# A graph layer's edge loop: windows of 16 to 80 nodes, sums zeroed by DMA, and three more copied columns on VectorE and ScalarE

## The chip, the core and the metric

The kernel runs on one core of one Trainium2 chip. The time is device microseconds of one launch. The core's engines work in parallel, each through its own list of instructions in order: PE (TensorE, matmul), DVE (VectorE), ACT (ScalarE), POOL (GpSimd) and SP (SyncE, which here only issues DMA). They wait for each other through semaphores. A "q" behind an engine's name, as in DVEq or SPq, means its queue: what is handled before the engine's arithmetic, such as register loads, waits and DMA issues.

## What is computed

The reference is one pre-normed layer of a graph network, with 12500 nodes of 48 values and 400000 edges of 32 values that are sorted by their target node `dst`:

```
h = jnp.maximum(_layernorm(x, axis=-1), 0.0)
x_i = h[dst]
x_j = h[src]
tmp = jnp.concatenate([x_i, x_j, edge_attr], axis=1)
h2 = jax.nn.relu(tmp @ W1 + b1)
msg = h2 @ W2 + b2
x = x + jax.ops.segment_sum(msg, dst, num_segments=12500)
```

The targets are drawn as 12500 u^2 with u uniform, so low nodes have many edges and high nodes few. The sources `src` are uniform.

## The kernel before

First `node_tables` (L102) normalizes the nodes and multiplies them by the two node parts of W1. That makes two tables in DRAM, `tab_a` for targets and `tab_b` for sources, 128 values a row. The table for sources is made a second time, turned, in the core's own memory: `bt`, 128 partitions with one column per node, written by `turn` (L296) in the loop's first iterations, three blocks of 1024 nodes an iteration.

The edges are then taken in 391 chunks of 1024, which are 8 tiles of 128 edges (`windows`, L230). A chunk's targets lie within 80 nodes (`W`). For each chunk:

- SP loads the edge values and, spread over 80 partitions, the target numbers (`lhs`, `row`, L354 and L356), and 80 rows of `tab_a` (`rhs`, L364).
- DVE compares the targets with the 80 node numbers (L379), which makes `lhs` a matrix with a one where an edge meets its target, and counts them in `deg`. It makes the same matrix with edges on partitions, `hot` (L389).
- PE multiplies `lhs` by `rhs` into `pre` (L400): target part and edge part of all 1024 edges. It adds the rows of the sources (L421), which come in one of three ways, below. ACT takes relu of it (`hid`, L437). PE folds the edges onto the chunk's 80 nodes (`p_g`, L445 and L448), and DVE adds that to a piece of the running sums `seg` (L460).

The rows of the sources come in three ways. POOL gathers most tiles from `tab_b` with one indirect DMA per tile of 128 (`gb`, L371; seven buffers of a chunk each). SP fetches the rows of some tiles one by one (`gs`, L289, 15 rows per iteration). And DVE and ACT copy single columns out of `bt` into a turned tile (`gt`, L348): 71 on DVE and 72 on ACT per iteration from iteration 5 on, so that 128 copies make a tile and 430 of the 3125 tiles come that way. A column's address is known only at run time; it is loaded from the table `cols` into the engine's registers by TENSOR_LOAD (L272), a few numbers at a time, ahead of the copies that use them. `PARTS` (L60) lists these parts: five on DVE with 8, 15, 16, 20 and 12 copies and six on ACT with 12, 8, 8, 20, 12 and 12, and `columns` (L325) rounds the number of loaded registers up to a multiple of four; the second part on DVE loads one more, the place of the seg add.

The sums: `seg` has two buffers of 1024 nodes. Twelve chunks make a group (`GQ`, L29; 33 groups and a bit), which uses one buffer. At a change of group DVE zeroes the other buffer with two memsets (L476), loads a number and copies 80 columns of sums over (L478). In the next group's first two iterations PE multiplies the old group's sums by W2 (`p_f`, L488 and L489), DVE adds them to the nodes' values `xseg` (L495), and SP stores those at the group's third (L499).

All runs in a hand-written order: the loop at L502 calls the steps of up to three chunks per iteration, and each engine takes its instructions in just that order. Iteration c prepares chunk c, multiplies chunk c-1 and folds chunk c-2.

Of the kernel before, what the change touches and what calls it, by code (L numbers as in the profile page):

```python
# [28 lines left out]
GQ = 12  # L29
OFF = -(NCH - 3) % GQ  # L30
L = 1024
FAR = L - W
END_L = 4 * W
MID = FAR / 2
BLK = 512
STORE = 2
# [7 lines left out]
HALF = (W - 1) / 2  # L44
# [7 lines left out]
TURNS = 3  # L52
BLOCKS = (NPAD + CE - 1) // CE
BUILD = (BLOCKS + TURNS - 1) // TURNS
COLS = BUILD
# [10 lines left out]
STRIP = 144  # L66
# [4 lines left out]
BASE = 0  # L71

BT0 = 16512
SEG0 = 161696
# [3 lines left out]
AT_PLACE, AT_SEG, SEG, NEXT = 16, 17, 18, 19  # L78
WIDTH = 20
# [13 lines left out]
EPS = 1e-5  # L93

# [135 lines left out]
def windows(nc, tc, gp, bt, ident, idx, raw, rhss, x_t, tab_a, tab_b, dst, edge_t, w2s, b2s,  # L230
            sources, out_t):
# [4 lines left out]
    with ExitStack() as es:  # L236
# [7 lines left out]
        wp = es.enter_context(tc.tile_pool(name="wp", bufs=3))  # L244
        ps_p = es.enter_context(tc.tile_pool(name="ps_p", bufs=2, space=PSUM))
        ps_g = es.enter_context(tc.tile_pool(name="ps_g", bufs=2, space=PSUM))
        ps_f = es.enter_context(tc.tile_pool(name="ps_f", bufs=1, space=PSUM))
        xp = es.enter_context(tc.tile_pool(name="xp", bufs=2))
# [4 lines left out]
        nc.vector.tensor_scalar_add(wnum, wrow, -HALF)  # L253
# [7 lines left out]
        gss = {}  # L261

        def group(c):

            return divmod(c + OFF, GQ)

        def begin(g):
            return max(0, g * GQ - OFF)

# [24 lines left out]
        bt_v = bt.rearrange("h (p r) -> h r p", r=NR)  # L294

        def turn(i):  # L296

            n = min(T, NR - i * T)
            p_t = ps_p.tile([P, T, HID], F32, name="pre")
            parts = p_t.rearrange("h (k q) p -> h k q p", k=2)  # L300
            for k in range(2):
                nc.tensor.matmul(
                    parts[:, k, : n // 2, :].rearrange("h q p -> h (q p)"), wb[:, k, :],
                    ht[: 2 * D, i * T // 2 : (i * T + n) // 2, :].rearrange("k g p -> k (g p)"),
                    start=True, stop=True,
                )
            nc.scalar.copy(
                bt_v[:, i * T : i * T + n, :].rearrange("h (q k) p -> h q k p", k=2),
                parts[:, :, : n // 2, :].rearrange("h k q p -> h q k p"),
            )  # L310
# [14 lines left out]
        def columns(c, part):  # L325
# [15 lines left out]
            for k, of in enumerate(got[:n]):  # L341
                j, e = divmod(first + k, P)
                if j not in gts:
                    gts[j] = gtc.tile([HID, P], F32, name="gt")
                of = of.with_bounds(
                    min_val=BT0, max_val=BT0 + 4 * (N - 1), guaranteed_mod_val=0, out_of_modulus=4
                ) - BT0
                copy(gts[j][:, e : e + 1], bt8[:, bass.ds(of, 4)].bitcast(F32))  # L348

        def prepare(c):  # L350
            n = min(T, NT - c * T)
            at = c * CE
            lhs = ld.tile([P, CE], F32, name="lhs")
# [3 lines left out]
                row[:, : n * P],  # L357
                dst[at : at + n * P].rearrange("(o e) -> o e", o=1).to_broadcast([W, n * P]),
            )
            m = max(0, min(RPART, len(BYROWS) * P - (c - ROWS0) * RPART)) if c >= ROWS0 else 0  # L360
            base, *nodes = numbers(c, BASE, 1 + m, mybir.EngineType.SP)
# [3 lines left out]
                rhs.bitcast(U8)[:W, :],  # L365
                taba8[bass.ds(base, 4 * HID * W)].rearrange("(w h) -> w h", w=W),
# [3 lines left out]
            for t in range(n - len(COLS_OF.get(c, ())) - (c in BYROWS) if c >= RAW else 0):  # L370
# [9 lines left out]
                lhs[:W, : n * P], row[:, : n * P], bw[:, c : c + 1], None,  # L380
                op0=ALU.is_equal, op1=ALU.add, accum_out=deg[:, :1],
# [3 lines left out]
        def compare(c):  # L385

            n = st[c]["n"]
            hot = wp.tile([P, T, W], F32, name="hot")
            nc.vector.tensor_tensor(  # L389
                hot[:, :n, :], wnum.unsqueeze(1).to_broadcast([P, n, W]),  # L390
                rel[:, c * T : c * T + n].unsqueeze(2).to_broadcast([P, n, W]), op=ALU.is_equal,
            )
            st[c]["hot"] = hot
# [46 lines left out]
        def fold(c):  # L440
            s = st[c]
            n = s["n"]
            p_g = ps_g.tile([HID, 2, W], F32, name="p_g")
# [4 lines left out]
            nc.tensor.matmul(p_g[:, 1, :], s["deg"], ident[:W, :W], start=True, stop=True)  # L448
            s["p_g"] = p_g

        def add(c):

            s = st.pop(c)
# [5 lines left out]
            to = segs[k].bitcast(U8)[:, :, bass.ds(at, 4 * W)].bitcast(F32)  # L459
# [4 lines left out]
        def segment_load(g):  # L464

            first, = numbers(begin(g), SEG, 1, mybir.EngineType.SP)
            xs[g] = xp.tile([D, L], F32, name="xseg")
            n = L if begin(g + 1) < NCH else END_L
            nc.sync.dma_start(xs[g][:, :n], x_t[:, bass.ds(node(first), n)])

        def segment_next(g):

            old, new = segs[g % 2], segs[(g + 1) % 2]
            if g > 0:
                for k in range(2):
                    nc.vector.memset(new[:, k, W:], 0.0)  # L476
            of, = numbers(begin(g), NEXT, 1, mybir.EngineType.DVE)
            nc.vector.tensor_copy(  # L478
                new[:, :, :W], old[:, :, bass.ds(of.with_bounds(min_val=0, max_val=FAR), W)]
            )  # L480
# [16 lines left out]
        def segment_store(g, n):  # L497
            first, = numbers(begin(g), SEG, 1, mybir.EngineType.SP)
            nc.sync.dma_start(out_t[:, bass.ds(node(first), n)], xs.pop(g)[:, :n])  # L499

        with tc.manual_schedule():
            for c in range(NCH + 2):  # L502
# [11 lines left out]
                if 0 <= c - 2 < NCH:  # L514
                    add(c - 2)
                    if k == GQ - 1:
# [17 lines left out]
                if k == GQ - 3 or c == NCH - 1:  # L534
# [13 lines left out]
                for i in range(c * TURNS, min((c + 1) * TURNS, BLOCKS)):  # L548
                    turn(i)
# [6 lines left out]
def general(nc, tc, bt, ident, x_t, tab_a, tab_b, src_it, dst_it, dst, edge_t, w1, w2s, b2s,  # L556
            accs, out_t):

    with ExitStack() as es:
# [97 lines left out]
        with tc.tile_pool(name="gfin", bufs=1) as fin, tc.tile_pool(  # L657
            name="g_f", bufs=1, space=PSUM
        ) as ps_f:
            for r0 in range(0, NR, 14):  # L660
                s = slice(r0, r0 + 14)
                got = []
                for k in range(GNACC):
                    a = fin.tile([P, 14, D], F32, name=f"a{k}")
# [7 lines left out]
                for r in range(14):  # L672
# [7 lines left out]
def tile_gnn_preln(  # L680
# [15 lines left out]
    ones: bass.AP,  # L696
    w1: bass.AP,
# [40 lines left out]
    rhss = [const.tile([P, HID], F32, name=f"rhs{k}") for k in range(3)]  # L738
    flag = const.tile([1, 1], I32, name="flag")
# [8 lines left out]
    gp = ctx.enter_context(tc.tile_pool(name="gp", bufs=7))  # L748

    with tc.tile_pool(name="keep", bufs=1) as keep, tc.tile_pool(  # L750
# [14 lines left out]
        def loads():  # L765
# [13 lines left out]
            nc.gpsimd.tensor_scalar_add(b0f, b0f, HALF)  # L779
# [19 lines left out]
        def squares():  # L799
            nc.scalar.activation(bt[:, :NT], rel, AF.Square)  # L800
# [4 lines left out]

        furthest = keep.tile([P, 1], F32, name="furthest")
# [4 lines left out]
        def most():  # L811
# [4 lines left out]
            nc.vector.tensor_scalar(furthest, furthest, HALF * HALF, None, op0=ALU.is_gt)  # L816
# [3 lines left out]
        def check():  # L820
# [7 lines left out]
            nc.vector.tensor_scalar_add(wcol, wcol, -HALF)  # L828
            nc.vector.tensor_scalar(bw, b0f[:W, :], wcol[:W, :], None, op0=ALU.add)

            nc.vector.tensor_scalar(cols, cols, 4, BT0, op0=ALU.mult, op1=ALU.add)
            rows_at = slice(BASE, BASE + 1 + RPART)
# [7 lines left out]
            at = last[:, :, AT_PLACE : AT_PLACE + 1]  # L840
            nc.vector.scalar_tensor_tensor(
                at, last[:, :, AT_SEG : AT_SEG + 1], -4.0, at, op0=ALU.mult, op1=ALU.add
            )
            at_place = slice(PLACE, PLACE + 1)
            nc.vector.scalar_tensor_tensor(
                cols[:, :, at_place], cols[:, :, at_place], 1.0, at, op0=ALU.mult, op1=ALU.add
            )

# [5 lines left out]
    with tc.If(outside == 0) as cmp:  # L854
        windows(nc, tc, gp, bt, ident, (srci, rel, bw, wrow, last, cols, degs), (xg, wb, ht), rhss,
                x_t, tab_a, tab_b, dst16, edge_t, w2s, b2s, sources, out_t)
# [78 lines left out]
```

## Time and profile before

| what | us |
|---|---|
| median of three runs | 3366.36 (3366.21 to 3367.52) |
| the profiled execution | 3372.65 |
| its span in the trace | 3370.8 |
| DVE busy, share of the span | 2800.1, 83% |
| ACT busy | 3035.6, 90% |
| PE busy | 2775.6, 82% |
| POOL busy | 2530.0, 75% |

In a row of groups stand the line, the engine, the instruction, what it writes and reads with partitions and elements, and how often; then busy time, the mean of one in ns, and the idle time of the engine just before, with what ended it. "Issue" there means that the engine waited for nothing that the profile shows. Register loads and waits are not counted as busy. Copies of one column overlap, so their mean duration is longer than the time from one to the next. In a timeline row stand start, length, engine, instruction, count, and in brackets the idle time before it. A row of windows has the stretch, its length, the busy time with the number of instructions in brackets, PE's granted clock, the DMA engines' busy share and GB/s.

### The profile page before, as it was taken

What the parts mean: (1) busy time and instruction counts of PE and PEld (TensorE: products, weight loads), DVE (VectorE), ACT (ScalarE), POOL (GpSimd) and SP (SyncE); (2) the same over time, 40 slices, a digit from 0 to 9 for tenths busy, and PEclk for the clock granted to TensorE, in tenths of its full rate; (3) what the DMA queues carried; (4) which work ended last, traced back from release to release, by engine and by line L of the source; (5) the groups of instructions that cost most, each with busy time, mean ns of one, the idle gap of its engine ahead of it and who ended that gap; (6) DMA issues with size and microseconds to landing.
All of it is one profiled execution on the core that took longest, in us unless ns stands there. A gap on an engine that the chain in (4) does not pass through costs nothing.

```text
span 3370.8 us, 115212 instructions
## 1 busy us (share of the span) xinstructions
PE 2775.6 (82%) x16394; PEld 2158.3 (64%) x16394; DVE 2800.1 (83%) x29140; ACT 3035.6 (90%) x28179; POOL 2530.0 (75%) x2670
## 2 busy tenths in 40 slices
PE   7987778888888888888887788888788788788777
PEld 6666666666666666666666666676666666666565
DVE  6588888888888888888888888888888888888876
ACT  5799998999998999998899999889998999999987
POOL 7677777777777777777777777777777777777776
PEclk9999998998898998988889999888998999899989
DMA  7433333333333333333333333333333333333333
GB/s 262 122 97 104 100 97 100 99 101 100 100 99 100 95 100 102 100 101 97 100 98 101 100 100 102 95 101 97 102 99 98 97 100 98 104 100 97 99 96 83
DMA packets 200234, 349.24 MB, mean 104 GB/s; under 512 B 69219, under 2 KB 107749, under 8 KB 198181
## 3 DMA queue, kind: packets, MB, share of 16 engines
q0 software_dynamic: 84800, 172.53, 18.9%
q1 hardware_dynamic: 114258, 169.09, 16.7%
q14 instruction: 634, 5.19, 0.5%
q8 instruction: 138, 2.26, 0.3%
q10 hardware_dynamic: 404, 0.17, 0.0%
HBM read 322.05 MB, written 22.07 MB: 102 GB/s over the span
## 4 chain that ended last, share of the span: by engine, by line
DVE 71%; issue 14%; PE 5%; DVEq 4%; POOL 2%; DMA 2%; ACT 0%; SPq 0%; POOLq 0%; ACTq 0%
DVE gt L348 47%; DVE lhs L379 12%; DVE hot L389 8%; DVEq L272 4%; DVE seg L460 2%; POOL gb L371 2%; PE pre L400 1%; PE p_g L445 1%; DVE xseg L495 1%; DVE seg L476 1%; DMA row<-in_dst 1%; PE p_f L488 1%; PE p_f L489 1%; DMA gb<-tab_b,srci 1%; PE p_n L195 1%
## 5 line engine op out<-in xcount | busy, mean ns | idle before, releaser
L371 POOL DMA_INDIRECT gb<-tab_b,srci x2618 | 2489.4, 951 | 812.7 <-issue 724.4
L348 ACT COPY gt<-bt 128x1 f32 x27705 | 2618.0, 188 | 63.9 <-issue 54.6
L348 DVE COPY gt<-bt 128x1 f32 x27335 | 1842.1, 144 | 463.3 <-issue 435.1
L400 PEld LDWEIGHTS pre<-rhs,lhs 112*128 112x128 f32 x6250 | 823.5, 208 | 277.1 <-issue 193.4
L400 PE MATMUL pre<-rhs,lhs 112*128 112x128 f32 x6250 | 841.5, 292 | 98.3 <-issue 56.7
L445 PE MATMUL p_g<-hot,hid 128*128 128x80 f32 x6250 | 794.0, 282 | 131.2 <-ACT hid L437 129.1
L445 PEld LDWEIGHTS p_g<-hot,hid 128*128 128x128 f32 x6250 | 758.4, 198 | 164.4 <-ACT hid L437 161.6
L421 PE MATMUL pre<-gb,ident 128*128 128x512 f32 (+2 forms) x1548 | 771.2, 627 | 34.3 <-DMA gb<-tab_b,srci 26.5
L437 ACT ACTIVATE hid<-pre 128x1024 f32<-128x1024 f32 x391 | 397.5, 1017 | 220.2 <-PE pre L421 205.8
L379 DVE TENSOR_SCALAR_CACHE_REDUCE lhs<-row,bw 80x1024 f32<-80x1024 int16 x391 | 494.6, 1265 | 14.8 <-DMA row<-in_dst 14.5
L421 PEld LDWEIGHTS pre<-gb,ident 128*128 128x128 f32 x1548 | 311.8, 225 | 281.0 <-issue 261.7
L421 PE MATMUL pre<-ident,gt 128*128 128x128 f32 x860 | 214.9, 336 | 261.7 <-DVE gt L348 234.7
L421 PEld LDWEIGHTS pre<-ident,gt 128*128 128x128 f32 x860 | 143.8, 210 | 291.5 <-issue 136.4
L389 DVE TENSOR_TENSOR hot<-wnum,rel 128x640 f32<-128x640 f32 x391 | 318.2, 814 | 0.0
L460 DVE TENSOR_TENSOR seg<-seg,p_g 128x160 f32 x391 | 121.5, 311 | 47.8 <-PE p_g L448 47.8
L448 PE MATMUL p_g<-ident,deg 80*128 80x80 f32 x782 | 156.4, 283 | 0.0
L448 PEld LDWEIGHTS p_g<-ident,deg 80*128 80x128 f32 x782 | 123.6, 198 | 0.0
L488 PE MATMUL p_f<-seg,w2s 128*48 128x512 f32 (+1 forms) x134 | 82.2, 700 | 44.3 <-DVE xseg L495 43.9
L489 PE MATMUL p_f<-seg,b2s 1*48 1x512 f32 (+1 forms) x134 | 76.2, 650 | 0.0
L488 PEld LDWEIGHTS p_f<-seg,w2s 128*48 128x48 f32 x134 | 12.3, 135 | 85.9 <-DVE xseg L495 60.0
L476 DVE MEMSET seg<- 128x944 f32 x64 | 54.1, 845 | 9.3
L489 PEld LDWEIGHTS p_f<-seg,b2s 1*48 1x48 f32 x134 | 11.3, 122 | 65.2 <-issue 65.2
(76 smaller groups left out, 429.0 us busy)
## 6 DMA issues: line engine op xcount, KB each, us to landing
gs<-tab_b SPq DMA_DIRECT2D x5760, 0.5 KB
row<-in_dst SPq DMA_DIRECT2D x390, 160.0 KB
lhs<-in_edge_t SPq DMA_DIRECT2D x390, 128.0 KB
gb<-tab_b,srci POOLq DMA_INDIRECT x2618
rhs<-tab_a SPq DMA_DIRECT2D x391, 40.0 KB
xseg<-in_x_t SPq DMA_DIRECT2D x33, 192.0 KB
out_x<-xseg SPq DMA_DIRECT2D x33, 192.0 KB
tab_b<-tab SPq DMA_DIRECT2D x3, 1280.0 KB
```

The costliest lines, as they stand in the source:

```text
L272: return nc.values_load_multi_w_load_instructions(table[c % P : c % P + 1, c // P, at : at + n], engines=[engine], min_val=0, max_val=1 << 23,
L348: copy(gts[j][:, e : e + 1], bt8[:, bass.ds(of, 4)].bitcast(F32))
L371: nc.gpsimd.indirect_dma_start(out=gb[:, t, :], out_offset=None, in_=tab_b[:, :], in_offset=bass.IndirectOffsetOnAxis(ap=srci[:, c * T + t ...
L379: nc.vector.tensor_scalar(lhs[:W, : n * P], row[:, : n * P], bw[:, c : c + 1], None, op0=ALU.is_equal, op1=ALU.add, accum_out=deg[:, :1],)
L389: nc.vector.tensor_tensor(hot[:, :n, :], wnum.unsqueeze(1).to_broadcast([P, n, W]), rel[:, c * T : c * T + n].unsqueeze(2).to_broadcast([P ...
L400: nc.tensor.matmul(pre[:, t, :], s["lhs"][:K, t * P : (t + 1) * P], s["rhs"][:K, :], start=t % BANK == 0, stop=False, skip_group_check=True,)
L421: nc.tensor.matmul(pre[:, t:e, :], lhsT, rhs, start=False, stop=True, skip_group_check=True)
L437: nc.scalar.activation(h[:, :n, :], s["pre"][:, :n, :], AF.Relu)
L445: nc.tensor.matmul(p_g[:, 0, :], s["h"][:, t, :], s["hot"][:, t, :], start=t == 0, stop=t == n - 1)
L448: nc.tensor.matmul(p_g[:, 1, :], s["deg"], ident[:W, :W], start=True, stop=True)
L460: nc.vector.tensor_add(to, to, s["p_g"])
L488: nc.tensor.matmul(p_f[:, :n], w2s, seg[:, 0, s], start=True, stop=False)
```

## The change

- *Spans.* The window of a chunk is 16, 32, 48, 64 or 80 nodes by its place in the edge list (`SPANS`). `hot`, the fold, the seg add, the row transfer, the `rhs` transfer and the partitions of the compare follow that width; the numbers are taken from the window's start, not its middle. `lhs` becomes three fixed buffers, zeroed once at the loop's start, and `rhs` too is zeroed at first. `hot` has two buffers for three. The test that all targets lie in their windows is made per span, by five ACT instructions for one.
- *Groups* have 12 to 103 chunks (`BEGINS`): 15 for 33. The old sums are zeroed by two DMAs on ACT's queue in the group's fifth and seventh iteration (`segment_clear`), not by DVE's memsets; the store comes at the fifth in place of the third.
- *Columns.* DVE's last part has 15 copies for 12, ACT's last too: 74 and 75 per iteration, from iteration 6 on. 447 tiles come that way.
- *Lane order.* `bt` has its columns in the order in which `turn` makes them, so that its copies write contiguous columns, and DVE turns node numbers into columns once, with five more instructions. The turns are spread 2, 2, 2, 2, 3, 2 over six iterations.
- *SP* loads 32 numbers in every second iteration in place of 16 in each.
- *Buffers.* `gb` has eight in place of seven.

```diff
-GQ = 12
+BEGINS = (0, 103, 147, 180, 208, 233, 255, 275, 294, 312, 329, 345, 360, 374, NCH - 5)
-END_L = 4 * W
+END_L = 5 * W
-STORE = 2
+STORE, CLEAR = 4, (4, 6)
+SPANS = ((16, 78), (32, 165), (48, 250), (64, 340), (W, NCH))
-TURNS = 3
+TURNS = (2, 2, 2, 2, 3, 2)
 PARTS = (
-    (True, 0, 8), (True, 8, 15), (True, 24, 16), (True, 40, 20), (True, 60, 12),
-    (False, 72, 12), (False, 84, 8), (False, 92, 8), (False, 100, 20), (False, 120, 12),
-    (False, 132, 12),
+    (True, 0, 8), (True, 8, 15), (True, 24, 16), (True, 40, 20), (True, 60, 15),
+    (False, 76, 12), (False, 88, 8), (False, 96, 8), (False, 104, 20), (False, 124, 12),
+    (False, 136, 15),
 )
...
+        lhss = [one.tile([P, CE], F32, name=f"lhs{k}") for k in range(3)]
+        for lhs in lhss:
+            nc.vector.memset(lhs[:W, :], 0.0)
...
             nc.scalar.copy(
-                bt_v[:, i * T : i * T + n, :].rearrange("h (q k) p -> h q k p", k=2),
+                bt[:, i * CE : i * CE + n * P].rearrange("h (q k p) -> h q k p", k=2, p=P),
...
-            base, *nodes = numbers(c, BASE, 1 + m, mybir.EngineType.SP)
+            if c % 2 == 0:
+                ahead[:] = numbers(c, 0, 2 * RPART + 2, mybir.EngineType.SP)
+            base, nodes = ahead[BASE + c % 2], ahead[c % 2 * RPART :][:m]
...
-                lhs[:W, : n * P], row[:, : n * P], bw[:, c : c + 1], None,
+                lhs[:w, : n * P], row[:w, : n * P], bw[:w, c : c + 1], None,
...
-                hot[:, :n, :], wnum.unsqueeze(1).to_broadcast([P, n, W]),
+                hot[:, :n, :], wnum[:, :w].unsqueeze(1).to_broadcast([P, n, w]),
...
-            to = segs[k].bitcast(U8)[:, :, bass.ds(at, 4 * W)].bitcast(F32)
+            to = segs[k].bitcast(U8)[:, :, bass.ds(at, 4 * w)].bitcast(F32)
...
-            if g > 0:
-                for k in range(2):
-                    nc.vector.memset(new[:, k, W:], 0.0)
...
+        def segment_clear(g, k):
+            nc.scalar.dma_start(
+                segs[g % 2][:, k, W:], zeros.unsqueeze(0).to_broadcast([P, L - W])
+            )
...
-                if g > 0 and k == STORE:
+                if g > 0 and k == (STORE if begin(g + 1) < NCH else 2):
                     segment_store(g - 1, L)
+                if g > 0 and begin(g + 1) < NCH and k in CLEAR:
+                    segment_clear(g - 1, CLEAR.index(k))
...
-    gp = ctx.enter_context(tc.tile_pool(name="gp", bufs=7))
+    gp = ctx.enter_context(tc.tile_pool(name="gp", bufs=8))
```

DVE's instructions of one iteration in the middle of a group, before, from the compare to the next one. `lhs`, `row` and `bw` belong to the compare, `cols` to the register loads, `gt` and `bt` to the column copies.

```order
L379 TENSOR_SCALAR lhs,deg_97<-row,bw 80x1024
L272 TENSOR_LOAD cols
L348 COPY gt<-bt 128x1 x8
L272 TENSOR_LOAD cols
L348 COPY gt<-bt 128x1 x15
L460 TENSOR_TENSOR seg_634<-seg_634,p_g 128x2x80
L272 TENSOR_LOAD cols
L348 COPY gt<-bt 128x1 x16
L389 TENSOR_TENSOR hot<-wnum,rel 128x640
L272 TENSOR_LOAD cols
L348 COPY gt<-bt 128x1 x20
L272 TENSOR_LOAD cols
```

The part that follows this last load has 12 copies before. The same place of the changed kernel, in a stretch with 32 nodes per window, from the last two loads of one iteration on:

```order
L276 TENSOR_LOAD cols
L350 COPY gt<-bt 128x1 x20
L276 TENSOR_LOAD cols
L350 COPY gt<-bt 128x1 x15
L387 TENSOR_SCALAR lhs_661,deg_100<-row,bw 32x1024
L276 TENSOR_LOAD cols
L350 COPY gt<-bt 128x1 x8
L276 TENSOR_LOAD cols
L350 COPY gt<-bt 128x1 x15
L471 TENSOR_TENSOR seg_652<-seg_652,p_g 128x2x32
L276 TENSOR_LOAD cols
```

The order and the five loads are the same; the last part has three copies more, and the compare, hot and the seg add are narrower.

DVE at a change of group, before, from the seg add on:

```order
L460 TENSOR_TENSOR seg_634<-seg_634,p_g 128x2x80
L476 MEMSET seg_635 128x944 x2
L272 TENSOR_LOAD last
L478 ISA
L478 COPY seg_635<-seg_634 128x2x80
L272 TENSOR_LOAD cols
L348 COPY gt<-bt 128x1 x16
```

And in the changed kernel:

```order
L471 TENSOR_TENSOR seg_653<-seg_653,p_g 128x2x32
L276 TENSOR_LOAD last
L486 ISA
L486 COPY seg_652<-seg_653 128x2x80
L276 TENSOR_LOAD cols
L350 COPY gt<-bt 128x1 x16
```

The two memsets are gone from DVE; the load and the copy stay. The zeroing stands on ACT, as a DMA behind the copies of an iteration.

More of the change, by code (lines that the diff above doesn't have):

```diff
@@ L261, in windows @@
         gss = {}
+        ahead = []
         def group(c):
-            return divmod(c + OFF, GQ)
+            g = max(0, sum(first <= c for first in BEGINS) - 1)
+            return g, c - BEGINS[g]
         def begin(g):
-            return max(0, g * GQ - OFF)
+            return BEGINS[g] if g < len(BEGINS) else NCH
         def numbers(c, at, n, engine, table=last):
@@ L547, in windows @@
                     sources()
[L548 to L549 removed]
+                if c < COLS:
+                    for i in range(sum(TURNS[:c]), sum(TURNS[: c + 1])):
+                        turn(i)
                 if c < PIECES:
```

141 lines of the change are left out of this document (86 added, 55 removed).

## The prediction, made before the change was run

> **What bounds the kernel now.** I read the page's engines and chain first, then the groups of instructions by line, then counts over the steady stretch, then the timeline of one loop iteration, and last the single register loads that the timeline leaves out.
>
> ```profile
> PE 2775.6 (82%) x16394; PEld 2158.3 (64%) x16394; DVE 2800.1 (83%) x29140; ACT 3035.6 (90%) x28179; POOL 2530.0 (75%) x2670
> DVE 71%; issue 14%; PE 5%; DVEq 4%; POOL 2%; DMA 2%; ACT 0%; SPq 0%; POOLq 0%; ACTq 0%
> ```
>
> ACT is the busiest engine, but the chain that ended last runs through DVE: 71% of it is DVE work, 14% "issue", in which an engine waited for nothing that the profile shows. The groups, with counts, busy time and idle time:
>
> ```profile
> L348 ACT COPY gt<-bt 128x1 f32 x27705 | 2618.0, 188 | 63.9 <-issue 54.6 <-ACT gt L348 1.0
> L371 POOL DMA_INDIRECT gb<-tab_b,srci x2618 | 2489.4, 951 | 812.7 <-issue 724.4 <-DMA gb<-tab_b,srci 45.5 <-PE pre L421 29.4
> L348 DVE COPY gt<-bt 128x1 f32 x27335 | 1842.1, 144 | 463.3 <-issue 435.1 <-ACT bt L307 1.2
> L389 DVE TENSOR_TENSOR hot<-wnum,rel 128x640 f32<-128x640 f32 x390 | 317.6, 814 | 0.0
> L460 DVE TENSOR_TENSOR seg<-seg,p_g 128x160 f32 x391 | 121.5, 311 | 47.8 <-PE p_g L448 47.8
> L495 DVE TENSOR_TENSOR xseg<-xseg,p_f 48x512 f32<-48x512 f32 x66 | 44.2, 670 | 7.0 <-PE p_f L489 7.0
> ...
> L389 DVE TENSOR_TENSOR hot<-wnum,rel 128x400 f32<-128x400 f32 x1 | 0.6, 564 | 0.0
> ```
>
> DVE's column copies have 435.1 us of "issue" idle before them; DVE waited for other engines little (47.8 us before the seg add, 7.0 before xseg). POOL shows no large wait either, so both are candidates. The next two rows count, over the same 3218 us, the instructions of L379 (two per chunk: compare and accumulator read) and the gathers of L371:
>
> ```profile
> 132.00:3350.00 3218.00, 489.29 (x768) 0.91 0.35 99
> ```
>
> ```profile
> 132.00:3350.00 3218.00, 2435.38 (x2562) 0.91 0.35 99
> ```
>
> So 384 iterations took 8.38 us each, and POOL issued a gather every 1.256 us. **POOL has no room**: in this stretch it goes from one gather to the next. All its gathers (min/median/max ns, first and last start):
>
> ```profile
> L371 POOL DMA_INDIRECT gb<-tab_b,srci x2618: 940/947/1924, 52.6 to 3353.5; - x187
> ```
>
> It starts at 52.6 us, before the loop, and so is ahead of the use of its rows; the last gather lies 17 us before the end, so the loop has worked that lead off by then. Two streams of nearly equal length thus stand beside each other: POOL's 2618 gathers, and the loop's 8.38 us, which is set by DVE. What sets DVE's 8.38 us is seen in one undisturbed iteration (start, length, instruction, idle before):
>
> ```profile
> 1461.62 1.27 DVE L379 TENSOR_SCALAR_CACHE_REDUCE lhs<-row,bw 80x1024 f32<-80x1024 int16 x1
> 1462.82 0.08 DVE L379 DVE_READ_ACCUMULATOR lhs<-row,bw 80x1 f32 x1
> 1462.82 1.63 DVE L348 COPY gt<-bt 128x1 f32 x23
> 1464.36 0.31 DVE L460 TENSOR_TENSOR seg<-seg,p_g 128x160 f32 x1
> 1465.18 1.06 DVE L348 COPY gt<-bt 128x1 f32 x16 [0.51 <-issue]
> 1466.16 0.81 DVE L389 TENSOR_TENSOR hot<-wnum,rel 128x640 f32<-128x640 f32 x1
> 1467.13 1.30 DVE L348 COPY gt<-bt 128x1 f32 x20 [0.16 <-issue]
> 1468.68 0.82 DVE L348 COPY gt<-bt 128x1 f32 x12 [0.24 <-issue]
> 1469.42 1.27 DVE L379 TENSOR_SCALAR_CACHE_REDUCE lhs<-row,bw 80x1024 f32<-80x1024 int16 x1
> ```
>
> Each group of copies waits for "issue" after the work before it has ended. The register loads of L272, which fetch the copies' column addresses, explain it. These are the five of that iteration (min/median/max ns, first and last start), for 8, 16, 16, 20 and 12 numbers:
>
> ```profile
> L272 DVEq TENSOR_LOAD <-cols x1: 601/601/601, 1461.3 to 1461.3; - x1
> L272 DVEq TENSOR_LOAD <-cols x1: 1100/1100/1100, 1462.3 to 1462.3; - x1
> L272 DVEq TENSOR_LOAD <-cols x1: 1095/1095/1095, 1464.0 to 1464.0; - x1
> L272 DVEq TENSOR_LOAD <-cols x1: 1351/1351/1351, 1465.7 to 1465.7; - x1
> L272 DVEq TENSOR_LOAD <-cols x1: 852/852/852, 1467.7 to 1467.7; - x1
> ```
>
> The load that starts at 1464.0 ends at 1465.1, and its 16 copies start at 1465.18; the one at 1465.7 ends at 1467.05, and its copies start at 1467.13; the one at 1467.7 ends near 1468.6, copies at 1468.68. So **DVE's instruction stream, not its arithmetic, is the bound**: the loads run one behind the other, nothing behind a load is handed out until it is done, and then some 31 to 37 ns per instruction go by until the next load. The five loads sum to 5.00 us of the 7.80 us from compare to compare; the other 2.80 us are 75 instructions (71 copies, the compare and its read, add, hot), 0.037 us each. The seg add and hot run in the shadow of the load behind them.
>
> [...]
>
> **The change, part by part.** The profiled execution took 3372.65 us, 6.3 above the median of 3366.36; I work out a difference and add it to the median.
>
> *74 and 75 columns.* DVE's last part grows from 12 to 15 copies, and its load from 12 to 16 numbers, since sizes are rounded up to four. The load goes from 0.852 to the 1.10 of the 16-number loads, +0.245; three more instructions at 0.037 add 0.11. That is +0.355 us per iteration, none of it under other work, over the 384 iterations that copy columns: **+136**. ACT copies three more too; from the row above a copy costs 2618.0/27705 = 0.0945 us, so 75 take 7.1 us, with hid about 8.1, under DVE's new 8.55: hidden with 0.4 us to spare. In return 17 tiles of 128 rows leave POOL (384 x 149 / 128 = 447 come by columns, for 385 x 143 / 128 = 430), 17 x 1.25 = 21 us of POOL; while DVE is the later stream that is worth nothing.
>
> *Narrower hot and seg add.* The mean width over the chunks is 45.9 in place of 80 (78 chunks at 16, 87 at 32, 85 at 48, 90 at 64, 51 at 80). At the two measured sizes of hot (814 ns for 640 elements, 564 for 400 in the last chunk) an element costs 1.04 ns, so hot shrinks by 0.28 us in the mean and the add by 0.07. Bounds: 0, if the load behind still ends when it did, and -0.35 x 391 = -137, if all is won. I take **0**, since the copies behind the add already wait 0.51 us and those behind hot 0.16. The compare keeps its 1024 elements per partition: 0. Smaller transfers and narrower fold matmuls lie beside DVE: 0.
>
> *Groups and their zeroing.* 33 changes of group become 14, and DVE's memsets go. One such iteration, the last:
>
> ```profile
> 3340.81 1.26 DVE L379 TENSOR_SCALAR_CACHE_REDUCE lhs<-row,bw 80x1024 f32<-80x1024 int16 x1
> 3344.10 1.83 DVE L476 MEMSET seg<- 128x944 f32 x2
> 3345.85 0.18 DVE L478 COPY seg<-seg 128x160 f32 x1
> 3345.94 1.05 DVE L348 COPY gt<-bt 128x1 f32 x16
> 3350.12 0.87 DVE L379 TENSOR_SCALAR_CACHE_REDUCE lhs<-row,bw 80x640 f32<-80x640 int16 x1
> ```
>
> It takes 9.31 us, some 1.1 over the 8.2 between the clean 7.80 and the mean 8.38: 33 x 1.1 = 36. The load of one number that places the group's copy stays:
>
> ```profile
> L272 DVEq TENSOR_LOAD <-last x33: 303/314/545, 125.8 to 3343.7; - x33
> ```
>
> 14 x 0.314 = 4, which leaves **-32**. The 66 xseg adds become 28, 38 x 0.67 = **-25** at most; if they too lie in a load's shadow it is 0. I take -25, because they come in front of a full queue. ACT issues 26 zeroing transfers; at the price of the first issue on ACT that is 10 us in all, inside ACT's spare time.
>
> ```profile
> 0.80 0.40 ACTq L756 DMA_DIRECT2D srci<-in_src_cols  x1
> ```
>
> *Waits and SP.* Separate waits ahead of the compare, SP's wait for its store of finished groups, and the compare's wait for its row:
>
> ```profile
> L379 DVEq EVENT_SEMAPHORE  x202: 21/21/50, 72.1 to 3340.4; - x101
> ```
>
> ```profile
> SPq L499 <- DVE xseg L495: 82.3, 10, 31.0
> ```
>
> ```profile
> DVE lhs L379 <- DMA row<-in_dst: 14.5, 7, 7.7
> ```
>
> With three fixed lhs buffers nothing but the row transfer is left to wait for, and the compare holds that wait itself: 202 x 0.05 us (21 ns and the handing out) is **-10**. SP, in order, stood before a store for up to 31.0 us with the next row transfers behind it; the store now comes two iterations later and half as often. Of DVE's 14.5 us of waiting for rows 7.7 belong to the start; the rest goes: **-7**. One load of 32 for two of 16 leaves SP as loaded as it was: 0.
>
> *Start.* Fewer turns per iteration, copies to contiguous lanes, three lhs memsets more.
>
> ```profile
> 84.54 1.02 ACT L437 ACTIVATE hid<-pre 128x1024 f32<-128x1024 f32 x1 [2.06 <-PE pre L411]
> 96.63 1.02 ACT L437 ACTIVATE hid<-pre 128x1024 f32<-128x1024 f32 x1 [3.68 <-PE pre L411]
> 100.86 1.98 PE L302 MATMUL pre<-ht,wb 96*128 96x512 f32 x4 [0.45 <-ACT bt L307]
> 127.82 0.95 POOL L371 DMA_INDIRECT gb<-tab_b,srci  x1 [12.98 <-PE pre L421]
> ```
>
> A start iteration takes 12.09 us, of which a turn is about 2 (the 1.98 of PE in the third row); one turn less in each of four saves 8, three turns later and the columns' start one iteration later give most of it back: **-3**, between -8 and +4. The eighth buffer takes most of POOL's 12.98 us wait, off the path.
>
> Sum: 136 - 32 - 25 - 10 - 7 - 3 = **+59**, so 3366.4 + 59 = **3425 us**.
>
> **Rivals.**
> *A, not slower: loads are no limit, POOL is.* If the narrower hot and add do shorten DVE's iteration, and the load of 16 hides as the copies in front of it are handed out, the loop gets faster than POOL, which then decides. POOL's stream loses 17 gathers (21 us) and about 10 of the 12.98 us wait: 3366 - 31 = 3335. It decides from a DVE iteration under about 8.3 us (the loop's 3218 us less 31, over 384). For it: POOL is as full as shown. Against it: the three places at which copies start 0.08 us behind their load. 0.12.
> *B, in between.* The mean iteration is 8.38, the clean one 7.80. If a third of the 0.58 us above it are waits that a slower stream or lighter transfers take up, 384 x 0.19 = 74 us go: 3351. Against it: DVE's named waits are small. 0.07, half of it above 3366.
> *C, slower still.* ACT's spare 0.4 us is thin, and a zeroing transfer waits on ACT's queue for the sums that read the old group, with copies behind it. 26 stalls of 2 us, passed on to PE and DVE, give 3425 + 52 = 3477. Against it: those sums are issued three iterations earlier. 0.04.
> That the spans fail, so that the general branch runs, would be far slower; a chunk at place c spans about 12500 (2c+1)/391^2 nodes by the reference, 12.7 at 77 and 63.9 at 390, under 16 and 80: below 0.01.
>
> **How the numbers follow.** Forecast 0.77, A 0.12, B 0.07, C 0.04. The forecast's own spread is 3390 to 3458 (xseg at 0 gives +25; part of hot won gives -30). To leave out no more than 0.2, the range reaches down over the upper half of B: 3362 to 3458. A run of this kernel can be told from no change from about 0.2%, 7 us, on: faster 0.15 (A and part of B), same 0.02, slower 0.83.
>
> **What would show it.** Right: loads of 16 numbers at 1.10 us in DVE's last part; "issue" idle before DVE's copies up from 435.1, by nearly what hot and the add lose in busy time; a mean iteration near 8.55; POOL waiting for buffers (PE pre L421) by tens of microseconds. Wrong: POOL still at 1.256 us per gather through the whole loop, with PE waiting for gb; or ACT with no idle before hid.

## The result, and the profile after

The changed kernel takes 3594.14 us (median of four runs, 3591.16 to 3597.66) against 3366.91 before: ratio 1.0672, 95% interval 1.0656 to 1.0689. The sign was forecast, the size was not: +227 us in place of +59, and above the range of 3362 to 3458. The profiled execution took 3592.45 us (span 3590.4). Beside fourteen of the eighteen experiment runs below the kernel before itself took 5330 to 5415 us, for a reason that stays open, so each run is compared only with the runs of before that stand beside it, and the steps are judged by the four beside which before took 3367.

The engines and the chain that ended last, from the page of the changed kernel:

```profile
PE 2875.8 (80%) x16276; PEld 2303.7 (64%) x16276; DVE 2654.8 (74%) x30112; ACT 3155.0 (88%) x29278; POOL 2493.9 (69%) x2655
DVE 55%; issue 17%; PE 9%; ACT 6%; SPq 5%; DVEq 3%; DMA 3%; ACTq 1%; POOL 0%
```

DVE's part of the chain fell from 71% to 55%. PE, ACT and SP's queue, with some 20% together, now take turns with it. The groups (count, busy us, mean ns, idle before and its main releaser):

```profile
L379 POOL DMA_INDIRECT gb<-tab_b,srci x2601 | 2454.4, 944 | 1015.1 <-issue 759.7
L350 ACT COPY gt<-bt 128x1 f32 x28800 | 2753.1, 187 | 276.7 <-issue 191.4
L350 DVE COPY gt<-bt 128x1 f32 x28416 | 1901.8, 143 | 699.8 <-issue 686.4
...
L471 DVE TENSOR_TENSOR seg<-seg,p_g 128x128 f32 (+4 forms) x391 | 94.1, 241 | 195.9 <-PE p_g L459 195.8
L398 DVE TENSOR_TENSOR hot<-wnum,rel 128x512 f32<-128x512 f32 (+4 forms) x391 | 207.0, 529 | 0.0
```

Two idle times have grown: ACT's copies have 276.7 us before them (before: 63.9), and DVE's seg add waits 195.8 us for PE (before: 47.8). The loop, from the seventh compare to the last, 768 instructions for 384 iterations:

```profile
125.60:3573.10 3447.50, 487.18 (x768) 0.83 0.32 85
```

That is 8.98 us per iteration, where 8.55 was forecast for the mean. Yet a usual iteration takes just that. One of them on DVE, its rows from one compare to the next (start, length, instruction, idle before):

```profile
605.87 1.26 DVE L387 TENSOR_SCALAR_CACHE_REDUCE lhs<-row,bw 16x1024 f32<-16x1024 int16 x1
...
608.59 0.18 DVE L471 TENSOR_TENSOR seg<-seg,p_g 128x32 f32 x1
609.46 1.06 DVE L350 COPY gt<-bt 128x1 f32 x16 [0.69 <-issue]
610.43 0.28 DVE L398 TENSOR_TENSOR hot<-wnum,rel 128x128 f32<-128x128 f32 x1
611.46 1.30 DVE L350 COPY gt<-bt 128x1 f32 x20 [0.75 <-issue]
613.31 1.18 DVE L350 COPY gt<-bt 128x1 f32 x15 [0.54 <-issue]
614.40 1.26 DVE L387 TENSOR_SCALAR_CACHE_REDUCE lhs<-row,bw 16x1024 f32<-16x1024 int16 x1
```

It takes 8.53 us, which is the median of all iterations too. The time is in the others: the 37 iterations longer than 9.2 us exceed 8.55 by 187 us in sum, and 169 us of it lie in 26 iterations of 10 to 21 us, one pair for each of the 13 groups whose sums are zeroed. This is ACT in one such pair:

```profile
1399.89 1.92 ACT L350 COPY gt<-bt 128x1 f32 x18
1411.22 0.34 ACTq L492 DMA_DIRECT2D seg<-in_zeros  x1
1412.48 2.69 ACT L350 COPY gt<-bt 128x1 f32 x28 [10.66 <-issue]
1415.08 1.01 ACT L446 ACTIVATE hid<-pre 128x1024 f32<-128x1024 f32 x1
```

ACT ends its copies at 1401.8, issues the zeroing transfer 9.4 us later, and only then goes on with copies and hid. PE needs that hid for p_g, and DVE's seg add needs p_g:

```profile
1420.23 0.22 DVE L471 TENSOR_TENSOR seg<-seg,p_g 128x64 f32 x1 [8.36 <-PE p_g L459]
```

What ACT waits for is on SP's queue in the same stretch:

```profile
1402.43 6.08 SPq L293 DMA_DIRECT2D gs<-tab_b  x15
1408.62 0.33 SPq L360 DMA_DIRECT2D lhs<-in_edge_t  x1
```

The link stands in the built program, which is the list of instructions with the semaphores that each waits for and raises. In it the completions of SP's and ACT's transfers count on the same eight semaphores in turn, and each of the 26 zeroing transfers waits for the last earlier transfer on its semaphore, which is one of SP's every time. The trace agrees: each of the 26 is issued 0.02 to 0.08 us after a landing on the semaphore that it raises. For this one ACT's row reads, in the order of the changed kernel (DMAHW1_49 is one of the eight):

```
L350 COPY gt<-bt 128x1 x15
L492 DMA seg_653<-in_zeros 128x944 [waits DMAHW1_49]
L276 TENSOR_LOAD cols
```

The awaited count is raised by SP's lhs transfer of chunk 157, while ACT is at the end of iteration 153: in the built program's order SP is four iterations ahead of ACT here, and three or four at all 26. On the chip SP was at chunk 156 when ACT came to its transfer at 1401.8. It first issued that chunk's 15 rows (6.08 us), issued the awaited transfer at 1408.62, and ACT went on at 1411.22, 2.6 us later. So 6.8 of the 9.4 us are SP's way there, and 2.6 go by until the transfer has landed. The same comparison for all 26 (issue of the awaited transfer of SP, issue of the zeroing transfer on ACT):

```
zeroing   awaited of SP        SP issues   ACT issues   behind
 1        gs row                 1014.99      1016.58     1.58
 2        gs row                 1043.72      1045.10     1.38
 3        lhs, chunk 157         1408.62      1411.22     2.61
 4        gs row                 1438.68      1440.27     1.59
26        gs row                 3513.81      3515.05     1.24
all 26: 1.23 to 1.66 behind a row of gs (0.5 KB), 2.46 to 3.29 behind lhs or row (128 KB)
```

ACT stands still before these 26 transfers for 1.2 to 10.8 us, 166 us in all. The waits of each engine, as "engine line <- releaser: us in total, times, longest":

```profile
ACT gt L350 <- issue: 191.4, 205, 12.1
ACT hid L446 <- PE pre L430: 79.9, 105, 4.6
ACT gt L350 <- DMA gs<-tab_b: 48.0, 5, 11.8
```

```profile
PE p_g L456 <- ACT hid L446: 425.5, 194, 14.4
```

```profile
POOL gb L379 <- PE pre L430: 234.9, 61, 13.4
```

Most of ACT's wait is put down to "issue": in the rows above, the wait of the zeroing transfer itself has no row. PE's wait for hid was a third of this before:

```profile
PE p_g L445 <- ACT hid L437: 129.1, 148, 2.2
```

POOL stands 234.9 us before buffers that PE has not freed.

### The profile page after: what moved, and what is told of

It reads as the page before. It is cut to its first block, busy times and chain, and to the rows that moved or that the text cites. A ratio compares the mean times of both kernels' runs of the same rounds, so it can differ in the third digit from the quotient of the medians.

```text
span 3590.4 us, 116932 instructions
## 1 busy us (share of the span) xinstructions
PE 2875.8 (80%) x16276; PEld 2303.7 (64%) x16276; DVE 2654.8 (74%) x30112; ACT 3155.0 (88%) x29278; POOL 2493.9 (69%) x2655
## 4 chain that ended last, share of the span: by engine, by line
DVE 55%; issue 17%; PE 9%; ACT 6%; SPq 5%; DVEq 3%; DMA 3%; ACTq 1%; POOL 0%
DVE gt L350 40%; DVE lhs L387 10%; ACT gt L350 4%; DVE hot L398 4%; PE p_g L456 3%; DVEq L276 3%; SPq L293 3%; PE pre L430 2%; PE pre L409 1%; DVE seg L471 1%; PE p_n L193 1%; ACT hid L446 1%; ACTq L276 1%; SPq L276 1%; DMA gs<-tab_b 1%
## 5 line engine op out<-in xcount | busy, mean ns | idle before, releaser
L350 ACT COPY gt<-bt 128x1 f32 x28800 | 2753.1, 187 | 276.7 <-issue 191.4
L350 DVE COPY gt<-bt 128x1 f32 x28416 | 1901.8, 143 | 699.8 <-issue 686.4
L456 PE MATMUL p_g<-hot,hid 128*128 128x64 f32 (+4 forms) x6250 | 844.0, 291 | 430.6 <-ACT hid L446 425.5
L456 PEld LDWEIGHTS p_g<-hot,hid 128*128 128x128 f32 x6250 | 813.4, 210 | 469.1 <-ACT hid L446 463.5
L430 PE MATMUL pre<-gb,ident 128*128 128x512 f32 (+2 forms) x1548 | 870.6, 700 | 0.0
L387 DVE TENSOR_SCALAR_CACHE_REDUCE lhs<-row,bw 64x1024 f32<-64x1024 int16 (+4 forms) x391 | 492.3, 1259 | 6.0 <-DMA row<-in_dst 6.0
L471 DVE TENSOR_TENSOR seg<-seg,p_g 128x128 f32 (+4 forms) x391 | 94.1, 241 | 195.9 <-PE p_g L459 195.8
L398 DVE TENSOR_TENSOR hot<-wnum,rel 128x512 f32<-128x512 f32 (+4 forms) x391 | 207.0, 529 | 0.0
L459 PE MATMUL p_g<-ident,deg 80*128 80x32 f32 (+4 forms) x782 | 169.6, 301 | 0.0
L502 PE MATMUL p_f<-seg,w2s 128*48 128x512 f32 (+1 forms) x58 | 35.6, 700 | 11.9 <-DVE xseg L509 11.4
```

Source lines behind the costliest of these rows:

```text
L387: nc.vector.tensor_scalar(lhs[:w, : n * P], row[:w, : n * P], bw[:w, c : c + 1], None, op0=ALU.is_equal, op1=ALU.add, accum_out=deg[:w, :1],)
L398: nc.vector.tensor_tensor(hot[:, :n, :], wnum[:, :w].unsqueeze(1).to_broadcast([P, n, w]), rel[:, c * T : c * T + n].unsqueeze(2).to_broad ...
L430: nc.tensor.matmul(pre[:, t:e, :], lhsT, rhs, start=False, stop=True, skip_group_check=True)
L456: nc.tensor.matmul(p_g[:, 0, :], s["h"][:, t, :], s["hot"][:, t, :], start=t == 0, stop=t == n - 1)
L459: nc.tensor.matmul(p_g[:, 1, :], s["deg"], ident[:W, :w], start=True, stop=True)
L471: nc.vector.tensor_add(to, to, s["p_g"])
```

## The experiments

The theory that they test: the 26 zeroing transfers on ACT's queue stop ACT, by the shared semaphores, and cost some 170 us; the three columns cost what VectorE's instruction stream says. The rivals: the columns make ACT late, and the stalls follow from that; the 12 MB of zeros or the sums that still read the old group are what ACT waits for; the lane order or the later waits cost on their own.

**One edit or both undone (before: 3367).** Memsets back on VectorE, no transfers on ACT:

```
+            if g > 0:
+                for k in range(2):
+                    nc.vector.memset(new[:, k, W:], 0.0)
...
-                if g > 0 and begin(g + 1) < NCH and k in CLEAR:
-                    segment_clear(g - 1, CLEAR.index(k))
```

and 71 and 72 columns:

```
-    (True, 0, 8), (True, 8, 15), (True, 24, 16), (True, 40, 20), (True, 60, 15),
+    (True, 0, 8), (True, 8, 15), (True, 24, 16), (True, 40, 20), (True, 60, 12),
...
-    (False, 136, 15),
+    (False, 136, 12),
```

First both undone, then the columns kept, then the transfers kept:

> The changed kernel with its 74 and 75 columns put back to 71 and 72, and with the sums zeroed by VectorE's memsets again instead of by transfers on ACT's queue; everything else stays as changed. Both costs that I name are gone, so on a chip on which the kernel before takes 3367 us I expect 3340 to 3355 us, slightly faster than before: what is left of the change are the fewer group changes, the fewer sums added for the statistics and the waits folded into the compare. The rival (the later waits and the different lane order cost on their own) says 3400 us or more.

> The changed kernel with VectorE's memsets in place of the transfers on ACT's queue, still with 74 and 75 columns. With both edits undone the kernel took 3344 us, 250 below the changed one. My theory gives the three columns 0.35 us in each of 384 iterations, 80 to 136 us, as far as VectorE's own stream of instructions sets the pace: 3420 to 3480 us here. The rival that the transfers alone make up the loss, and that the columns lie in spare time, says 3345 to 3360 us.

> The changed kernel with 71 and 72 columns, the transfers on ACT's queue kept. If the stall at each of the 26 transfers is a wait of its own, whatever the length of an iteration, it costs the 120 to 187 us that the trace of the changed kernel shows: 3465 to 3530 us. If ACT's shorter iterations take the stalls up (the rival: ACT is late only because it copies three more columns), 3345 to 3380 us.

| zeroing by | 71, 72 columns | 74, 75 columns | columns cost |
|---|---|---|---|
| VectorE's memsets | 3344.44 (0.9929, 0.9912 to 0.9945) | 3423.98 (1.0175, 1.0158 to 1.0192) | 79.5 |
| transfers on ACT | 3516.69 (1.0445, 1.0428 to 1.0462) | 3594.14 (1.0672, 1.0656 to 1.0689) | 77.5 |
| transfers cost | 172.3 | 170.2 | |

(In brackets the ratio to before and its interval.) The two edits add up: neither makes the other dearer or cheaper, so the rival that ACT stalls because it copies three more columns falls. With 71 and 72 columns all 26 transfers again follow an awaited one of SP, by 1.20 to 2.00 us, and PE waits for hid as long as in the changed kernel:

```profile
PE p_g L456 <- ACT hid L446: 455.6, 189, 18.7
```

Nothing else in the change costs on balance: with both undone the kernel is 0.7% faster than before. With the columns alone DVE is the bound that the prediction describes, and ACT's waits for issue are back at 63.8 us. In this run, the chain, ACT and PE:

```profile
DVE 72%; issue 20%; PE 4%; DVEq 4%; ACT 1%; DMA 0%; ACTq 0%; SPq 0%; POOL 0%
```

```profile
ACT gt L350 <- issue: 63.8, 198, 0.5
```

```profile
PE pre L430 <- DVE gt L350: 272.7, 204, 3.2
PE p_g L456 <- ACT hid L446: 173.3, 187, 2.1
...
PE pre L430 <- DMA gb<-tab_b,srci: 5.5, 4, 2.6
```

With both undone a second bound comes in beside DVE: POOL. The chain, PE's waits and POOL's gathers (min/median/max ns, first and last start):

```profile
DVE 44%; issue 19%; POOL 15%; PE 11%; DMA 4%; ACT 3%; DVEq 2%; ACTq 0%; SPq 0%; POOLq 0%
```

```profile
PE pre L430 <- DMA gb<-tab_b,srci: 184.8, 115, 4.3
PE pre L430 <- DVE gt L350: 125.7, 117, 2.9
```

```profile
L379 POOL DMA_INDIRECT gb<-tab_b,srci x2619: 940/944/1904, 53.5 to 3329.7; - x188
```

2619 gathers from 53.5 to 3329.7 are one every 1.251 us almost without a pause, and PE waits 184.8 us for them, 5.5 us with the three columns more. VectorE's stream would allow the forecast's 8.55 - 0.355 = 8.20 us per iteration, and the median iteration is 8.18. The mean is longer, 3200.9/384 = 8.34, and PE waits for rows 115 times:

```profile
124.40:3325.30 3200.90, 487.19 (x768) 0.87 0.33 87
```

This is rival A's floor.

**A transfer of one number.** The memsets are back, and at the places of the zeroing stands

```
-                segs[g % 2][:, k, W:], zeros.unsqueeze(0).to_broadcast([P, L - W])
+                speck, zeros[:1].rearrange("(o e) -> o e", o=1)
```

> The changed kernel with VectorE's memsets, and at the places of the 26 zeroing transfers a transfer of a single number on ACT's queue into a tile that nothing reads. If the size of the transfer or the sums that still read the old group make ACT wait, the stalls go: as with the memsets alone (3420 to 3480 us). If any transfer that ACT issues there waits for transfers that SP issues only chunks later, since both queues count on the same semaphores, the stalls stay: 3560 to 3610 us.

3604.59 us (1.0707, 1.0689 to 1.0725): 180.6 above the memsets alone, for 26 transfers of 4 bytes into a tile that nothing reads. The bytes and the readers of the old sums are out as causes; what costs is that ACT issues a transfer at these places. All 26 again follow an awaited transfer of SP by 1.23 to 3.48 us. ACT's waits, and the transfers themselves:

```profile
ACT gt L351 <- DMA speck<-in_zeros: 157.6, 21, 12.7
```

```profile
L496 ACTq DMA_DIRECT2D speck<-in_zeros x26: 456/457/548, 1017.2 to 3526.1; - x26
```

No run gave ACT's transfers semaphores of their own. That it is the shared semaphore is read from the built program, from the landings in the trace of the changed kernel, and from the 26 times in each of the three kernels above that issue from ACT.

**The runs beside which before took 5330 to 5415 us.** They are four sets, each with its own runs of before. There the copies of VectorE and ScalarE start far more slowly one behind the other. In the kernel with both edits undone, from 1500.1 to 1506.6 us, one or two of DVE's start every 0.7 us. DVE waits there for issue

```profile
DVE gt L350 <- issue: 2217.9, 3447, 1.5
```

where it waits, in the run at 3344,

```profile
DVE gt L350 <- issue: 581.1, 1230, 1.2
```

and ACT waits 1738.0 us in place of 59.7. In five more of these runs DVE's wait is 2205.6 to 2356.8 us. So what these runs say of columns holds for that pace alone. First the two edits and the zeroing by SP:

```
-            nc.scalar.dma_start(
+            nc.sync.dma_start(
                 segs[g % 2][:, k, W:], zeros.unsqueeze(0).to_broadcast([P, L - W])
```

> The changed kernel with the old sums zeroed by VectorE's two memsets at a change of group again, and no DMA on ScalarE's queue. Theory (a clear holds ScalarE for about 7 us, because its DMA must wait for a transfer of SP's that lies chunks ahead; 26 clears make up some 187 us above the clean iteration of 8.53): 3594 - 187 + 13 changes of group x 1.1 = about 3420, no ScalarE stall of 10 us, mean iteration 8.55 to 8.6. Rival (ScalarE with 75 copies is simply too slow, or the three more columns cost more than was reckoned): 3560 or more. Rival (the zeroing DMA's bytes or the sums it waits for): also about 3420, told apart by the next run and by a small DMA later.

> The changed kernel with the same 26 zeroing DMAs issued by SP in place of ScalarE. Theory (the wait lies in ScalarE's queue, behind a transfer that SP has not issued yet): SP's own transfers are in SP's order, so no such wait; about 3410 to 3430. Rival (the 472 KB transfers themselves, or the wait for the old group's sums, cost the time): stays near 3590, or SP's row transfers come late and VectorE's compare waits for them, over 3500.

> The changed kernel with 71 and 72 column copies per iteration as before (loads of 12 numbers in the last part of VectorE and ScalarE), all else as changed, the clears still on ScalarE. Theory (each iteration costs 0.355 us more by VectorE's longer register load and three more copies): 3594 - 137 = 3457, clean iteration 8.16 to 8.2; the 26 stalls stay. Rival (columns are hidden, the clears are all of it): 3590. Rival (ScalarE's thin slack is what the stalls come from): the stalls go too, about 3350.

> The changed kernel with both undone: memsets on VectorE and 71 and 72 columns. Theory: the loop needs 384 x 8.17 + 125 + 17 = 3280, less than GpSimd's 2618 gathers x 1.25 from 55 us on, so GpSimd is the bound: 3340 to 3355, PE waiting for gathered rows late in the loop. Rival (the two costs are not separate, or something else in the change is slow): over 3380. Rival (narrower hot and seg add gain time by themselves on VectorE, 137 us): cannot show here, as GpSimd ends last either way.

Before 5330.14; then 5490.22 with memsets, 5494.84 with SP's transfers, 5521.23 with 71 and 72 columns, 5401.37 with memsets and 71 and 72. None of the expected times came out, in this set and in the three below, but differences can be read: transfers on ACT cost 120 us (5521 - 5401), the same transfers on SP nothing against memsets. Then three of the edits again, and the transfer of one number:

> As e1, measured anew on a chip on which the kernel before takes its usual time: VectorE's memsets in place of the 26 zeroing DMAs on ScalarE's queue. Theory (each clear holds ScalarE for about 7 us): about 3420. Rival (three more columns or ScalarE's thin slack cost it all): 3560 or more.

> As e3, measured anew: 71 and 72 column copies, clears still on ScalarE. Theory (0.355 us per iteration by VectorE's register load of 16 numbers and three copies): about 3457, the stalls at the clears stay. Rival (columns are hidden): 3590. Rival (the stalls come from ScalarE's thin slack): about 3350.

> As e4, measured anew: memsets on VectorE and 71 and 72 columns. Theory: the loop falls below GpSimd's stream, so GpSimd's 2618 gathers x 1.25 us bound it: 3340 to 3355. Rival (something else in the change is slow): over 3380.

> VectorE's memsets do the zeroing, and at the places of the 26 clears ScalarE issues a DMA of one number into a tile that nothing reads. Theory (the stall is the wait of any DMA on ScalarE's queue for an earlier transfer of SP's on the same semaphore): the stalls stay, 3590 to 3610. Rival (the 472 KB of the zeroing transfer or the sums that it must wait for): no stalls, about 3420.

Before 5399.07; then 5559.22, 5615.99, 5470.34, 5653.86: ACT's transfers cost 146 us (5616 - 5470), one number 95 us above memsets. The third set asks for the parts of the columns and for hot. The edits are SP's zeroing with 71 and 75 columns; a load of 16 numbers of which 12 are copied (with memsets, 71 and 72 columns); and hot 80 nodes wide everywhere (with memsets, 74 and 75):

```
-            size = -(-n // 4) * 4 if place is None else place + 1 - at
+            size = -(-n // 4) * 4 + 4 * (at == 60) if place is None else place + 1 - at
```

```
-            n, w = st[c]["n"], span(c)
+            n, w = st[c]["n"], W
```

> The changed kernel with its 26 zeroing transfers issued from SP's queue instead of ACT's; the bytes and the places in the loop stay. If only ACT's waiting for SP's transfers costs the time, it goes, and VectorE's 13 pairs of memsets go with it against the run with memsets (3424 us): 3405 to 3425 us. If the 12 MB of zeros cost by themselves, or SP comes late by them, 3450 to 3600 us.

> The zeroing transfers on SP's queue, 71 columns on VectorE as before the change, 75 on ACT as changed. If only VectorE's three columns cost time, and with them gone POOL's gathers set the pace (3344 us with 71 and 72 columns, 2619 gathers of 1.25 us), the nine gathers that ACT's three columns save give 3325 to 3345 us. If ACT's three copies cost as much as VectorE's, 3370 to 3400 us.

> 71 and 72 columns and VectorE's memsets (3344 us), but VectorE's last load of an iteration takes 16 numbers in place of 12, of which 12 are copied: the load's longer time alone. With the columns VectorE sets the pace at 3424 us, and the three copies are 0.11 us of 384 iterations, 42 us; the load alone so gives 3424 - 42, 3370 to 3390 us. If only the copies cost, 3340 to 3350 us.

> VectorE's memsets and 74 and 75 columns (3424 us), but the comparison that makes hot is 80 nodes wide in every chunk, as before the change; TensorE still reads the narrow part. It is 110 us more of VectorE's busy time. My theory says that the compare lies beside the register load behind it, which is longer: 3415 to 3440 us. The rival, that VectorE's busy time is what counts, says 3520 to 3540 us.

Before 5414.69; then 5590.42, 5589.97, 5497.16, 5585.40. Two of these were run once more:

> The zeroing transfers on SP's queue, 71 columns on VectorE as before the change, 75 on ACT as changed. If ACT's three columns lie in spare time, and POOL's gathers set the pace once VectorE's three columns are gone (3344 us with 71 and 72 columns and memsets), the nine gathers of 1.25 us that ACT's columns save, 11 us, and the 13 pairs of memsets saved give 3325 to 3345 us. If ACT's three copies cost as much as VectorE's, 3370 to 3400 us; if the 12 MB of zeros cost by themselves or SP comes late by them, 3400 us and more.

> 71 and 72 columns and VectorE's memsets (3344 us), but VectorE's last load of an iteration takes 16 numbers in place of 12, of which 12 are copied: the load's longer time alone. With the columns VectorE sets the pace at 3424 us, and the three copies are 0.11 us of 384 iterations, 42 us; the load alone so gives 3424 - 42, 3370 to 3390 us. If only the copies cost, 3340 to 3350 us.

Before 5398.11; then 5563.88 and 5479.62. At this pace three columns less on VectorE change nothing (5590.42 and 5589.97), the longer load alone stands at 1.0151 and 1.0147 of before, beside 1.0147 and 1.0138 for the kernel without it, and the kernel with ACT's three columns is 84 us slower than that with 72 (5564 - 5480; the two also differ in the zeroing, which cost nothing on SP, and in the load). So there ACT's copies carry the price and VectorE's do not, the opposite of what the trace at 3424 shows. Hot at full width costs nothing (5585, with memsets, against 5590, with SP's transfers). These runs cannot decide how the 80 us split at the normal pace, and no run was made of it there: that VectorE's columns and not ACT's are what binds is read from the trace (PE waits 272.7 us for VectorE's columns; the stream's iteration of 8.53), not shown by a run. Zeroing from SP's queue was not run at that pace either.

## Why the prediction was wrong in size

**The step that failed** is "ACT issues 26 zeroing transfers; at the price of the first issue on ACT that is 10 us in all, inside ACT's spare time". The issue itself is cheap (0.34 us each, 9 us in all), but a wait stands in front of it. The transfers cost 170 us in all, and as the memsets that they replace are 13 pairs at the forecast's 1.1 us, some 14 us, each transfer costs (170 + 14)/26 = 7.1 us on the mean; the transfer of one number, beside which the memsets stay, gives 180.6/26 = 6.9. The trace has the same size: ACT stands still for 166 us in all, and the 26 long iterations hold 169 us above 8.55. The price was taken from ACT's first transfer (0.40 us at 0.80), which in the built program waits for nothing; the loop of before has no transfer on ACT at all. Rival C had the place and the way on to PE and DVE right (chance 0.04), but the wrong reason, the sums that read the old group, and 2 us in place of 7: 52 us instead of 184.

**The columns.** The kernel without ACT's transfers takes 3423.98 us. The forecast's sum for it is 3425 plus the 14 us of memsets that the sum had removed, so the sum is within 15 us. Its parts are less sure than that: 0.34 us of the median iteration, below, is 131 us for the columns, which leaves -74 for the rest where the forecast has -63, but only the sum of the two was measured. The load of 15 copies is as forecast (min/median/max ns), 16 numbers in 1.15 us where 1.10 was said:

```profile
L276 DVEq TENSOR_LOAD <-cols x1: 1150/1150/1150, 612.1 to 612.1; - x1
```

The prediction's undisturbed iteration of 7.80 us is one of the shortest of before, whose median is 8.24, and between the loads of before 35 to 43 ns per instruction go by in the median, not 31 to 37; neither moves the sum. The median iterations of the kernels with and without the columns are 8.52 and 8.18 us; the difference of 0.34 is nearly the forecast's 0.355. But undoing the columns gave 80 us and not 136, since PE then waits for POOL's rows. Rival A's floor of 3335 us is 9 us from the 3344 measured; its reason, that the loads hide, is not what happens, since the copies still start behind their loads: the first one 0.09 us after the load's end in the median, before and in the changed kernel. (These copies use the very numbers that the load fetches. That they start behind it does not show that an instruction without that need would wait too, as the prediction's "nothing behind a load is handed out" says.)

**Narrower hot and seg add at nothing:** the trace bears it out. They lose 318.2 - 207.0 and 121.5 - 94.1, 139 us of busy time, and with both edits undone "issue" idle before the copies rises by 581.1 - 435.1 = 146. In the iteration above, copies stand 0.69 us after the add and 0.75 after hot where it was 0.51 and 0.16. One run tells it too: with the columns alone the median iteration is 8.52 us where windows have 16 nodes and 8.51 where they have 64, though hot takes 0.28 us in the one stretch and 0.68 in the other (8.59 with 80 nodes and 0.81). The compare keeps its time, as said: 1.26 us in the mean on 16 partitions, 1.27 on 80 before.

**Groups, xseg, waits, start (-77 in sum):** not told apart. With both edits undone, memsets included, 22 us are left of them, and POOL's floor hides the rest. DVE's wait for rows fell from 14.5 to 6.0 us as said. The start gave nothing: the seventh compare begins at 125.6 in place of 132.1, but the iteration behind it takes 14.5 us, and the eighth stands at 140.2 against 139.9.

**POOL:** 17 gathers fewer (2601 for 2618), and tens of microseconds of waiting for buffers in the kernel without ACT's transfers (59.9 us), as said; the 234.9 us of the changed kernel are ACT's stalls passed on.

## What to carry to other kernels

A transfer moved to another engine's queue can cost that engine more than its issue, here some 7 us where the issue takes 0.34: read in the built program which semaphore it waits for and whose earlier transfer raises it, and ask when that queue gets there on the chip. Here a queue that runs behind held an engine that is busy for 88% of the span at each of 26 transfers, of 472 KB or of 4 bytes. And when two streams are nearly equal, work out a floor for both: here 80 us came back of the 136 added to DVE's, since POOL's then set the pace.

## What the runs showed of the hardware that was not expected

A transfer of 4 bytes from ACT's queue cost as much as one of 472 KB (180.6 and 170 + 14 us for 26). The zeroing transfers, 12 MB in all, had no price of their own that the runs could tell.
